# A fused attention block with its block products cut into four column tiles

## The chip, the cores and the metric

The kernel runs on one core of a Trainium2 chip. The metric is the device time of one execution in microseconds (us). Before the change three runs gave 721.99, 722.10 and 722.43 us; their median is 722.1 us. A difference of 0.2% (1.4 us) is about what a measurement of this kernel can tell from no change.

## The reference

The input `x` has 8 batches of 512 positions by 512 channels; `tokens` is one conditioning row for each batch. There are 16 heads of 32 channels.

```python
Q = split_heads(x @ Wq.T + bq);  tQ = split_heads(tokens @ Wq.T + bq)
K = split_heads(x @ Wk.T + bk);  tK = split_heads(tokens @ Wk.T + bk)
V = split_heads(x @ Wv.T + bv)
scores = einsum('bhqd,bhkd->bhqk', Q + tQ, K + tK) / sqrt(32)
out = einsum('bhqk,bhkd->bhqd', softmax(scores, axis=-1), V)
return x + merge_heads(out)
```

Everything is float32.

## The kernel before

**Work units.** A unit `t` is one batch and one group of four heads, 32 units in all (`T`), four to a batch. The four heads of a group lie on the 128 partitions, 32 channels each. A unit needs its q and k turned so that channels lie on partitions (`qkT`, 128 x 512), v with positions on partitions (`vs`), and the row maxima of its scores.

**Four steps for a unit.** The main loop (line 806) runs over the units and does four steps for each, one per chunk `kc` of 128 keys. The instructions of TensorE (PE), VectorE (DVE), ScalarE (ACT) and GpSimd (POOL) run in the order in which they are written; only the order of SyncE's DMA queue (SP) is left to the framework. Each step holds, on PE in this order:

1. `exponentials(t, kc)`: four bf16 matmuls (line 570) that put the negated row maxima into four PSUM banks, and on top of them four float32 matmuls k times q, one for each head (line 573). Each uses 32 rows of the array, so the four heads' row tiles (32\*128) run side by side. ACT turns the banks into `e` (line 584).
2. `row_max(t+1, qc)`: four float32 matmuls q times k of the next unit, again 32\*128 row tiles, into four other banks (line 499). DVE takes the negated maxima of heads 0 and 1 one by one (line 490, 128x512 each) and those of heads 2 and 3 in one instruction over two banks (line 508, 128x1024). ACT then sums the exponentials of these banks for the softmax denominators (`denominators`, line 518), one instruction for each head, which waits for that head's maximum.
3. In steps 0, 2 and 3: half of a projection of the next batch (q in step 0, k in step 2, v in step 3). In step 1: `weighted`, the product of `e` and v for the unit before (line 589, column tiles 128\*32: 128 rows, 32 columns, the four heads side by side), a small product with 16 columns (line 620) and the output.

**A projection in seven products.** A 256-wide half of a projection is a 2 x 2 block product. It is done with seven block products instead of eight, from sums and differences of blocks of x and of W (`xc`, `wc`), listed in `MADE_OF`. `first_products` (odd units) does products 1, 6, half of 2, and 7; `other_products` (even units) does 4, 5, the other half of 2, and 3. Either is seven float32 matmuls of 128 x 128 weights by 256 columns, written at lines 403 (v) and 406 (q, k). The trace lists each float32 matmul as two passes, each with its own weight load: 14 passes for a half. There are 92 such halves in the kernel: 30 for q, 30 for k, 32 for v.

**The small work on a projection.** In `first_products` ACT copies product 1 from PSUM to its place in SBUF (`m1`, line 438), ahead of the denominators. Later DVE adds it to products 6 and 2 (lines 444, 445) and adds product 7 (line 426 for v, 429 for q and k). The last of these releases the bank of product 1. After step 2's maxima, POOL splits them into three bf16 parts (`split_max`, lines 532 to 535) and SP turns them by a DMA transpose (`turn_max`, line 544) for the `exponentials` of the next unit.

**PSUM.** Eight banks are handed out by a table, `TURNS`, one row for a step; `banks(i)` is the i-th bank of the row, `advance()` goes to the next row. A matmul into a bank waits until its last reader is done; the wait sits on its weight load.

Of the kernel before, what the change touches and what calls it, by code (L numbers as in the profile page):

```python
# [12 lines left out]
ALU = mybir.AluOpType  # L13
AX = mybir.AxisListType
# [3 lines left out]
def kernel(  # L18
# [49 lines left out]
    T = B * G  # L68
    HS = S // 2
# [175 lines left out]
    for i in range(NS):  # L245
        r = slice(i * BL, (i + 1) * BL)
# [142 lines left out]

    def block_of_x(b, i, kc, at):  # L390
        f = MADE_OF[i - 1][1]
        if isinstance(f, int):
            return xc[:, f, kc, at]
        off = HS * (f == "22")
        return xT[b][:, kc + 2 * (f != "11"), at.start + off : at.stop + off]

    def product(n, b, u, i, pt, kcs=(0, 1)):

        for kc in kcs:
            w = block_of_w(n, i, u, kc)  # L400
            if n == "v":
                xb = block_of_x(b, i, kc, slice(u * P, (u + 1) * P))
                nc.tensor.matmul(pt, xb, w, start=(kc == kcs[0]), stop=(kc == kcs[-1]))  # L403
            else:
                xb = block_of_x(b, i, kc, slice(0, HS))
                nc.tensor.matmul(pt, w, xb, start=(kc == kcs[0]), stop=(kc == kcs[-1]))  # L406

    def twice(a):
        return a.unsqueeze(1).broadcast_to([P, 2, HS])

    def halves(a):
        return a.rearrange("p (h s) -> p h s", h=2)


    def parts_of(n, b, u):

        if n == "v":
            v = vs[b % 2]
            return v[:, u::2, :HS], v[:, u + 2, :HS], v[:, u::2, HS:], v[:, u + 2, HS:]
        o = pair_of(b * G + u * 2, n)  # L420
        return halves(o[:, 0, :]), o[:, 0, HS:], halves(o[:, 1, :]), o[:, 1, HS:]

    def plus(n, b, u, g, o, pt, rest):

        if n == "v":
            nc.vector.tensor_tensor(o, pt, rest, ALU.add)
        else:
            add = tok[:, "qk".index(n), u * 2 + g, b : b + 1]
            nc.vector.scalar_tensor_tensor(o, pt, add, rest, ALU.add, ALU.add)

    def first_products(n, b, u, dens, small, at, first=0):


        one_, two_ = banks(first), banks(at)
        c1, c12, c2, c22 = parts_of(n, b, u)
        m1 = c2[:, 0, :]
        product(n, b, u, 1, one_[:, :HS])
        nc.scalar.copy(m1, one_[:, :HS])
        dens()
        product(n, b, u, 6, two_[:, :HS])  # L440
        small()
        product(n, b, u, 2, two_[:, HS:], (0,))
        product(n, b, u, 7, one_[:, HS:])
        nc.vector.tensor_tensor(c12, two_[:, :HS], m1, ALU.add)
        nc.vector.tensor_tensor(c1[:, 0, :], two_[:, HS:], m1, ALU.add)
        plus(n, b, u, 1, c22, one_[:, HS:], c12)

    def other_products(n, b, u, dens, small, at):

        dens()  # L450
        one_, two_ = banks(at[0]), banks(at[1])
        product(n, b, u, 4, one_[:, :HS])
        product(n, b, u, 5, one_[:, HS:])
        small()
        product(n, b, u, 2, two_[:, :HS], (1,))
        product(n, b, u, 3, two_[:, HS:])
        c1, c12, c2, c22 = parts_of(n, b, u)
        nc.vector.tensor_tensor(c12, one_[:, HS:], c12, ALU.add)
        nc.vector.tensor_tensor(c2, halves(one_), twice(c22), ALU.add)
        plus(n, b, u, 0, c1, halves(two_), c1)  # L460
        if n != "v":
            for g in range(2):
                qkT[n, b * G + u * 2 + g] = pair_of(b * G + u * 2, n)[:, g, :]

    def project_pair(n, b, r, dens, small, at):

        if b >= B:
            dens()
            small()
        else:  # L470
            (first_products, other_products)[r % 2](n, b, r // 2, dens, small, at)


    nmax = {}
# [4 lines left out]
            nmax[t] = op.tile([P, NS, HG, 1], F32, tag="nmax", name=f"nmax_{t}", bufs=3)  # L479
            sums[t] = op.tile([P, NS, HG, 1], F32, tag="sums", name=f"sums_{t}", bufs=3)  # L480

    def row_max(t, qc):
        if t >= T:
            return
        open_max(t)
        for j in range(HG):
            row_scores(t, qc, j, banks(HG + j))
        if t < T - 2 or t * NS + qc == T * NS - 1:
            for j in range(2):
                nc.vector.tensor_reduce(  # L490
                    nmax[t][:, qc, j : j + 1, 0], banks(HG + j), AX.X, ALU.max, negate=True
                )
        else:
            row_max_of(t, qc, 0, banks(HG, 2))
        row_max_of(t, qc, 1, banks(HG + 2, 2))

    def row_scores(t, qc, j, pt):
        r = slice(j * HD, (j + 1) * HD)
# [8 lines left out]
    def row_max_of(t, qc, pr, pt):  # L507
        nc.vector.tensor_reduce(  # L508
            nmax[t][:, qc, pr * 2 : pr * 2 + 2, 0], pt, AX.X, ALU.max, negate=True
        )  # L510
# [15 lines left out]
    def split_max(t, on=nc.gpsimd):  # L526

        if t >= T:
            return
        m, sp = nmax[t], split[t % 2]  # L530
        rest = op.tile([P, NS, HG, 1], F32, tag="rest", name=f"rest_{t}")
        on.tensor_copy(sp[:, :, :, 0:1], m)
        on.tensor_tensor(rest, m, sp[:, :, :, 0:1], ALU.subtract)
        on.tensor_copy(sp[:, :, :, 1:2], rest)
        on.tensor_tensor(sp[:, :, :, 2:3], rest, sp[:, :, :, 1:2], ALU.subtract)
# [3 lines left out]
    def turn_max(t):  # L539

        if t >= T:
            return
        maxT[t] = op.tile([P, S], BF16, tag="maxT", name=f"maxT_{t}")
        nc.sync.dma_start_transpose(
            maxT[t].rearrange("p (c q) -> p c q", c=NS),
            split[t % 2].rearrange("p c h e -> p (c h e)"),
        )
# [202 lines left out]

    turn[0] = 13
    row_max(0, 0)
    turn_w("v", [1, 2, 3])
    combine_w("v")
# [51 lines left out]
    for t in range(T - 3):  # L806
        b, r = divmod(t, G)

        exponentials(t, 0)
        row_max(t + 1, 1)  # L810
        of = ((t - 1) // G + 1, (t - 1) % G)
        dens = lambda: denominators(t + 1, 1)
        if t:
            project_pair("q", *of, dens, nothing, 1 if r % 2 else (0, 3))
        else:
            first_products("v", 0, 0, dens, nothing, 1)
            turn_x(NC + 2)
            load_residual(1)
        turn_x(t + NC + 3)
        advance()  # L820

        exponentials(t, 1)
        row_max(t + 1, 2)
        dens = lambda: denominators(t + 1, 2)
        if t:
            dens()
            weighted(
                t - 1, banks(0), banks(1), lambda: combine_x(b + 1, r) if r < 2 else None
            )
        else:  # L830
            dens()
            other_products("v", 0, 0, nothing, nothing, (0, 2))
        advance()

        exponentials(t, 2)
        row_max(t + 1, 3)
        split_max(t + 1)
        turn_max(t + 1)
        dens = lambda: denominators(t + 1, 3)
        if t:  # L840
            project_pair("k", *of, dens, nothing, 1 if r % 2 else (0, 3))
        else:
            first_products("v", 0, 1, dens, nothing, 1)
            combine_x(1, 0)
        if t:
            load_residual(t + 1)
        advance()

        exponentials(t, 3)
        row_max(t + 2, 0)  # L850
        dens = lambda: denominators(t + 2, 0)

        project_pair("v", *of, dens, nothing, 1 if r % 2 else (0, 2))
        advance()


# [55 lines left out]
    t = T - 3  # L912
# [21 lines left out]
    t = T - 2  # L934
# [15 lines left out]
    pa, rest = banks(2), [1, 2, 3]  # L950
# [8 lines left out]
    t = T - 1  # L959
# [47 lines left out]
    b, g = divmod(t, G)  # L1007
# [55 lines left out]
```

## Time and profile before

| what | value |
|---|---|
| median of three runs | 722.1 us |
| the profiled execution: its time, its span | 722.59 us, 720.8 us |
| PE busy | 714.2 us (99% of the span), 5296 matmul passes |
| PE weight loads busy | 401.3 us (56%) |
| ACT busy | 617.3 us (86%) |
| DVE busy | 528.0 us (73%) |
| POOL busy | 176.3 us (24%) |
| mean granted TensorE clock | 0.999 |

In the views, `32*128` in front of a shape is rows times columns of the array that a matmul uses, then follow the moving operand's shape and the number of instructions. PEld is the weight load. In a timeline the first number is the start in us from the start of the span and the second the length; a group's length includes the last one's pipeline, so that groups seem to overlap: the pace is read from the differences of starts.

### The profile page before, as it was taken

How to read it: one execution, taken by the hardware profiler on the slowest of the kernel's cores; microseconds unless marked ns; L12 is line 12 of the kernel's file. 1: busy time of each engine (PE TensorE's matmuls, PEld its weight loads, DVE VectorE, ACT ScalarE, POOL GpSimd, SP SyncE). 2: the span in 40 equal slices, each digit the busy share in tenths (PEclk: the TensorE clock that was granted, in tenths of full speed). 3: DMA queues.
4: the chain of work that ended last, by engine and by line, in shares of the span. 5: the costliest groups of instructions: out<-in, count | busy, mean ns of one | idle time of the engine just before them, and what ended most of it. 6: DMA issues, size and time to landing. Idle time of an engine off the chain costs nothing.

```text
span 720.8 us, 14892 instructions
## 1 busy us (share of the span) xinstructions
PE 714.2 (99%) x5296; PEld 401.3 (56%) x5296; DVE 528.0 (73%) x834; ACT 617.3 (86%) x1539; POOL 176.3 (24%) x275
## 2 busy tenths in 40 slices
PE   9999999999999999999999999999999999999997
PEld 7566555565555566555565555565555565555532
DVE  4798777777768777677776877777767767767777
ACT  2589989999899998989999889998989989889674
POOL 3712221122221122221122221122221122221351
PEclk9999999999999999999999999999999999999999
DMA  6733321222322222321322321323201222211211
GB/s 177 110 60 62 53 41 30 49 44 46 53 35 36 50 41 49 53 41 28 51 41 49 52 40 27 53 37 52 38 16 23 38 38 38 37 21 19 37 32 29
DMA packets 223358, 32.91 MB, mean 46 GB/s; under 512 B 221610, under 2 KB 222122, under 8 KB 223284
## 3 DMA queue, kind: packets, MB, share of 16 engines
q1 hardware_dynamic: 221524, 30.92, 25.3%
q10 hardware_dynamic: 1760, 1.05, 0.5%
q8 instruction: 41, 0.67, 0.4%
q14 instruction: 33, 0.27, 0.1%
HBM read 19.75 MB, written 8.39 MB: 39 GB/s over the span
## 4 chain that ended last, share of the span: by engine, by line
PE 97%; DVE 2%; issue 1%; DMA 1%; DVEq 0%
PE psum L406 27%; PE psum L499 16%; PE psum L589 15%; PE psum L403 14%; PE psum L573 14%; PE psum L570 5%; PE psum L350 2%; DVE acc L863 1%; PE psum L889 1%; DMA w_q<-in_L_cond_Wq_dram 1%; PE psum L266 0%; DVE acc L861 0%; PE psum L311 0%; PE psum L667 0%; PE psum L599 0%
## 5 line engine op out<-in xcount | busy, mean ns | idle before, releaser
L518 ACT ACTIVATE dead<-psum,nmax 128x512 f32<-128x512 f32 x480 | 327.6, 702 | 5.1 <-DVE nmax L490 3.1
L584 ACT ACTIVATE e<-psum 128x512 f32<-128x512 f32 x488 | 252.0, 602 | 64.2 <-PE psum L573 63.9
L490 DVE TENSOR_REDUCE nmax<-psum 128x1 f32<-128x512 f32 x240 | 154.5, 686 | 143.1 <-PE psum L499 143.1
L508 DVE TENSOR_REDUCE nmax<-psum 128x2 f32<-128x1024 f32 x130 | 157.7, 1214 | 2.8 <-PE psum L499 2.7
L499 PE MATMUL psum<-kT,qT 32*128 32x512 f32 x1024 | 143.9, 605 | 0.0
L646 POOL TENSOR_TENSOR res<-res,recs 128x512 f32<-128x512 f32 x30 | 31.5, 1049 | 432.1 <-DVE res L645 432.1
L573 PE MATMUL psum<-qT,kT 32*128 32x512 f32 x976 | 125.5, 587 | 0.0
L589 PE MATMUL psum<-e,v 128*32 128x512 f32 x1024 | 121.2, 596 | 0.0
L518 ACT ACTIVATION_READ_ACCUMULATOR dead<-psum,nmax 128x1 f32 x480 | 105.2, 219 | 0.0
L499 PEld LDWEIGHTS psum<-kT,qT 32*128 32x128 f32 x1024 | 59.8, 183 | 58.1 <-ACT dead L518 26.4
L589 PEld LDWEIGHTS psum<-e,v 128*32 128x32 f32 x1024 | 26.6, 110 | 65.1 <-issue 37.6
L573 PEld LDWEIGHTS psum<-qT,kT 32*128 32x128 f32 x976 | 48.6, 185 | 2.2
L403 PE MATMUL psum<-wc_v,xc 128*128 128x256 f32 x192 | 49.3, 379 | 0.0
L570 PE MATMUL psum<-maxT,onesb 3*128 3x512 bf16 x488 | 48.1, 384 | 0.0
L406 PE MATMUL psum<-xc,wc_k 128*128 128x256 f32 x180 | 46.2, 379 | 0.0
L406 PE MATMUL psum<-xc,wc_q 128*128 128x256 f32 x180 | 46.2, 379 | 0.0
L570 PEld LDWEIGHTS <-onesb 3*128 3x128 bf16 x488 | 12.3, 90 | 57.2 <-issue 57.2
L173 POOL TENSOR_TENSOR xr<-xr,bvs 128x512 f32<-128x512 f32 x31 | 39.4, 1272 | 18.7 <-DMA x<-in_x_dram 12.0
L403 PEld LDWEIGHTS psum<-wc_v,xc 128*128 128x128 f32 x192 | 36.5, 190 | 5.0
L647 POOL TENSOR_TENSOR res<-res,xr 128x512 f32<-128x512 f32 x30 | 38.2, 1273 | 2.4
L403 PE MATMUL psum<-wT_v,xT 128*128 128x256 f32 x128 | 37.1, 392 | 0.0
L406 PEld LDWEIGHTS psum<-xc,wc_k 128*128 128x128 f32 x180 | 34.2, 190 | 4.7
(165 smaller groups left out, 791.2 us busy)
## 6 DMA issues: line engine op xcount, KB each, us to landing
xr<-in_x_dram SPq DMA_DIRECT2D x124, 64.0 KB, 2.4
out_dram<-res SPq DMA_DIRECT2D x122, 64.0 KB, 1.9
x<-in_x_dram SPq DMA_DIRECT2D x112, 64.0 KB, 2.4
w_q<-in_L_cond_Wq_dram SPq DMA_DIRECT2D x4, 256.0 KB, 4.4
w_v<-in_L_cond_Wv_dram SPq DMA_DIRECT2D x16, 64.0 KB, 2.4
w_k<-in_L_cond_Wk_dram SPq DMA_DIRECT2D x16, 48.0 KB, 2.3
x<-in_x_dram ACTq DMA_DIRECT2D x2, 256.0 KB, 3.9
x<-in_x_dram SPq DMA_DIRECT2D x2, 256.0 KB, 4.2
```

The lines of the kernel that those rows point to most:

```text
L173: nc.gpsimd.tensor_tensor(xr[t], xr[t], bias, ALU.add)
L403: nc.tensor.matmul(pt, xb, w, start=(kc == kcs[0]), stop=(kc == kcs[-1]))
L406: nc.tensor.matmul(pt, w, xb, start=(kc == kcs[0]), stop=(kc == kcs[-1]))
L490: nc.vector.tensor_reduce(nmax[t][:, qc, j : j + 1, 0], banks(HG + j), AX.X, ALU.max, negate=True)
L499: nc.tensor.matmul(pt, qkT["q", t][r, qc * P : (qc + 1) * P], qkT["k", t][r, :], start=True, stop=True,)
L508: nc.vector.tensor_reduce(nmax[t][:, qc, pr * 2 : pr * 2 + 2, 0], pt, AX.X, ALU.max, negate=True)
L518: nc.scalar.activation(dead, banks(HG + j), AF.Exp, bias=nmax[t][:, qc, j, :], accum_out=sums[t][:, qc, j, :],)
L570: nc.tensor.matmul(bank[j], onesb[r, :], maxT[t][r, :], start=True, stop=False)
L573: nc.tensor.matmul(bank[j], qkT["k", t][r, kc * P : (kc + 1) * P], qkT["q", t][r, :], start=False, stop=True,)
L584: nc.scalar.activation(e[:, i, :], bank[pr * 2 + i], AF.Exp)
L589: nc.tensor.matmul(pt[j * HD : (j + 1) * HD, :], vs[b % 2][:, kc, (g * HG + j) * HD : (g * HG + j + 1) * HD], es[t, kc, j // 2][:, j % 2, ...
L647: nc.gpsimd.tensor_tensor(y, y, xr.pop(t), ALU.add)
```

## The change

`product` issues, instead of one matmul of 128 weight columns, four matmuls of 32 weight columns with the same moving operand, each into its 32 partitions of the same bank. `first_products` in the main loop has DVE copy product 1 instead of ACT, and DVE takes the last two maxima of that step only after this copy, one by one; in step 2 the split and the turn of the maxima follow them. The two `first_products` of unit 0 and those ahead of the loop keep ACT's copy. In even units the order stays as it was.

```diff
@@ product
-                xb = block_of_x(b, i, kc, slice(u * P, (u + 1) * P))
-                nc.tensor.matmul(pt, xb, w, start=(kc == kcs[0]), stop=(kc == kcs[-1]))
+                still, moving = block_of_x(b, i, kc, slice(u * P, (u + 1) * P)), w
             else:
-                xb = block_of_x(b, i, kc, slice(0, HS))
-                nc.tensor.matmul(pt, w, xb, start=(kc == kcs[0]), stop=(kc == kcs[-1]))
+                still, moving = w, block_of_x(b, i, kc, slice(0, HS))
+            for j in range(HG):
+                r = slice(j * HD, (j + 1) * HD)
+                nc.tensor.matmul(
+                    pt[r], still[:, r], moving, start=(kc == kcs[0]), stop=(kc == kcs[-1])
+                )
@@ first_products
-    def first_products(n, b, u, dens, small, at, first=0):
+    def first_products(n, b, u, dens, small, at, first=0, held=None):
...
         product(n, b, u, 1, one_[:, :HS])
-        nc.scalar.copy(m1, one_[:, :HS])
+        if held:
+            nc.vector.tensor_copy(m1, one_[:, :HS])
+            held()
+        else:
+            nc.scalar.copy(m1, one_[:, :HS])
         dens()
@@ project_pair
-    def project_pair(n, b, r, dens, small, at):
+    def project_pair(n, b, r, dens, small, at, held):
+        if r % 2:
+            held()
         if b >= B:
             dens()
             small()
-        else:
-            (first_products, other_products)[r % 2](n, b, r // 2, dens, small, at)
+        elif r % 2:
+            other_products(n, b, r // 2, dens, small, at)
+        else:
+            first_products(n, b, r // 2, dens, small, at, 0, held)
@@ row_max
+    def one_max(t, qc, j, pt):
+        nc.vector.tensor_reduce(
+            nmax[t][:, qc, j : j + 1, 0], pt, AX.X, ALU.max, negate=True
+        )
+
-    def row_max(t, qc):
+    def row_max(t, qc, hold=False):
...
-        row_max_of(t, qc, 1, banks(HG + 2, 2))
+        last, both = [banks(HG + 2), banks(HG + 3)], banks(HG + 2, 2)
+
+        def held():
+            if hold and t < T - 2:
+                for j in range(2):
+                    one_max(t, qc, 2 + j, last[j])
+            else:
+                row_max_of(t, qc, 1, both)
+
+        if hold:
+            return held
+        held()
+        return nothing
@@ the main loop, step 0 (step 3 likewise)
-        row_max(t + 1, 1)
+        held = row_max(t + 1, 1, r % 2)
...
-            project_pair("q", *of, dens, nothing, 1 if r % 2 else (0, 3))
+            project_pair("q", *of, dens, nothing, 1 if r % 2 else (0, 3), held)
@@ the main loop, step 2
-        row_max(t + 1, 3)
-        split_max(t + 1)
-        turn_max(t + 1)
+        rest = row_max(t + 1, 3, r % 2)
+
+        def held():
+            rest()
+            split_max(t + 1)
+            turn_max(t + 1)
+
...
-            project_pair("k", *of, dens, nothing, 1 if r % 2 else (0, 3))
+            project_pair("k", *of, dens, nothing, 1 if r % 2 else (0, 3), held)
```

The product matmuls grow from 644 to 2576, in 14 x 4 passes instead of 14 for a half. 42 copies of product 1 move from ACT to DVE, and 42 maxima over two banks become 84 over one bank. On SP the framework puts two DMAs of `xr` instead of one ahead of the DMA transpose of the maxima in odd units.

More of the change, by code (lines that the diff above doesn't have):

```diff
@@ L489, in row_max @@
             for j in range(2):
-                nc.vector.tensor_reduce(
-                    nmax[t][:, qc, j : j + 1, 0], banks(HG + j), AX.X, ALU.max, negate=True
-                )
+                one_max(t, qc, j, banks(HG + j))
         else:
             row_max_of(t, qc, 0, banks(HG, 2))
-        row_max_of(t, qc, 1, banks(HG + 2, 2))
+        last, both = [banks(HG + 2), banks(HG + 3)], banks(HG + 2, 2)
[9 more added lines that the diff above has]
+        return nothing
     def row_scores(t, qc, j, pt):
@@ L835 @@
         exponentials(t, 2)
-        row_max(t + 1, 3)
-        split_max(t + 1)
-        turn_max(t + 1)
+        rest = row_max(t + 1, 3, r % 2)
[3 more added lines that the diff above has]
+            turn_max(t + 1)
         dens = lambda: denominators(t + 1, 3)
         if t:
-            project_pair("k", *of, dens, nothing, 1 if r % 2 else (0, 3))
+            project_pair("k", *of, dens, nothing, 1 if r % 2 else (0, 3), held)
         else:
+            held()
             first_products("v", 0, 1, dens, nothing, 1)
@@ L849 @@
         exponentials(t, 3)
-        row_max(t + 2, 0)
+        held = row_max(t + 2, 0, r % 2)
         dens = lambda: denominators(t + 2, 0)
-        project_pair("v", *of, dens, nothing, 1 if r % 2 else (0, 2))
+        project_pair("v", *of, dens, nothing, 1 if r % 2 else (0, 2), held)
         advance()
```

## The prediction

> **What bounds the kernel.** I read the page first: busy shares, then the chain that ended last.
>
> ```profile
> PE 714.2 (99%) x5296; PEld 401.3 (56%) x5296; DVE 528.0 (73%) x834; ACT 617.3 (86%) x1539; POOL 176.3 (24%) x275
> ...
> PE 97%; DVE 2%; issue 1%; DMA 1%; DVEq 0%
> PE psum L406 27%; PE psum L499 16%; PE psum L589 15%; PE psum L403 14%; PE psum L573 14%; PE psum L570 5%; PE psum L350 2%; DVE acc L863 1%; PE psum L889 1%; DMA w_q<-in_L_cond_Wq_dram 1%; PE psum L266 0%; DVE acc L861 0%; PE psum L311 0%; PE psum L667 0%; PE psum L599 0%
> ```
>
> PE is the bound nearly everywhere, and 41% of the chain (L406 and L403) are the products that the change cuts. What a pass costs, and what lies between passes, is seen in the timeline of PE from 300 to 318 us:
>
> ```profile
> 301.05 1.12 PE L499 MATMUL psum<-kT,qT 32*128 32x512 f32 x8
> 302.10 1.13 PE L403 MATMUL psum<-wT_v,xT 128*128 128x256 f32 x4
> 303.07 1.03 PE L403 MATMUL psum<-wc_v,xc 128*128 128x256 f32 x4
> 303.93 0.59 PE L403 MATMUL psum<-wT_v,xT 128*128 128x256 f32 x2
> 304.36 1.03 PE L403 MATMUL psum<-wc_v,xc 128*128 128x256 f32 x4
> 305.32 0.40 PE L570 MATMUL psum<-maxT,onesb 3*128 3x512 bf16 x4
> ...
> 306.41 1.11 PE L499 MATMUL psum<-kT,qT 32*128 32x512 f32 x8
> ...
> 311.75 1.03 PE L499 MATMUL psum<-kT,qT 32*128 32x512 f32 x8
> 312.71 1.07 PE L589 MATMUL psum<-e,v 128*32 128x512 f32 x8
> 313.59 0.23 PE L620 MATMUL psum<-apart,modulo 128*32 128x16 f32 x8
> 313.65 2.76 PE L589 MATMUL psum<-e,v 128*32 128x512 f32 x24
> 316.35 0.40 PE L570 MATMUL psum<-maxT,onesb 3*128 3x512 bf16 x4
> ```
>
> From the differences of starts: four passes of 256 columns take 0.97 us when they are the first after L499 (302.10 to 303.07) and 0.863 later (303.07 to 303.93; 216 ns a pass). The column tiles of L589 are the model for the changed products. Their four heads run side by side: 24 passes, six rounds of four, in 2.69 us; 430 ns a round of 512 columns, so 215 for 256. **The cut therefore saves nothing on a pass**, a pass in four column tiles being one round.
>
> The grouped lines, shapes kept apart, say the same of the entry: a group that holds first passes has a longer mean (25 ns over four passes, 12.5 over eight: about 104 ns for each first one).
>
> ```profile
> L403 PE MATMUL psum<-wc_v,xc 128*128 128x256 f32 x192 | 49.3, 379 | 0.0
> L403 PE MATMUL psum<-wT_v,xT 128*128 128x256 f32 x128 | 37.1, 392 | 0.0
> L403 PE MATMUL psum<-wT_v,xc 128*128 128x256 f32 x64 | 18.1, 405 | 0.0
> ```
>
> Last the timeline of all engines around 306.4, for what PE waits for:
>
> ```profile
> 306.11 0.22 ACT L518 ACTIVATION_READ_ACCUMULATOR dead<-psum,nmax 128x1 f32 x1
> 306.38 0.21 PEld L499 LDWEIGHTS psum<-kT,qT 32*128 32x128 f32 x4 [0.22 <-ACT dead L518]
> 306.41 0.68 PE L499 MATMUL psum<-kT,qT 32*128 32x512 f32 x4
> ```
>
> ACT ends its last denominator at 306.33; PE's weight load for that bank goes 0.05 later, too late to hide under the pass before, and L499 takes 1.04 us (306.41 to 307.44) instead of 0.956 (311.75 to 312.71).
>
> **Part 1, the column tiles.** *Entry:* 104 ns of a 128-column weight load are exposed at the first pass (0.967 - 0.863). For L589 eight passes from 312.710 to 313.593 are two rounds in 0.883, against 0.859: 24 ns, a 32-column load. Saved: 80 ns. *Exit:* from the last four product passes to L570 0.96 us (304.36 to 305.32) less 0.863, 0.096; from the last six rounds of L589 to L570 2.694 less 6 x 0.4295, 0.117. The four tiles start some 7 ns apart, and the last one ends 20 ns later. Lost: 20 ns. *Between passes:* four 32-column loads (110 ns each, side by side) must hide under 213 ns of matmul instead of 427. The 128-column load of 190 ns does so now. I take nothing. Net 60 ns for each of the 92 halves: **5.5 us**.
>
> One kind does not pass it all on. In step 2 of even units DVE's last operation (L429, 751 ns) releases the bank that L499 waits for; it starts 0.09 after the last product pass, and DVE's own queue would let it start only 0.04 earlier. Off: 15 x 0.02, **0.3 us**.
>
> **Part 2, ACT loses its copy, DVE gets it.** Starts of L499 to the next group, over the main loop: 0.955 where nothing is late; 1.057 after a q `first_products` (14 times), 1.051 after k (14), 1.037 after v (16, 14 of them changed), and 1.040 after k `other_products` (15, DVE's case above, which stays). The first three end in ACT, as in the last fence. In place of a copy and four denominators ACT has only the denominators. The copy takes 0.27 us of ACT's time from start to next start (330.19 to 330.46); in a v step ACT also waits 0.1 for product 1. ACT ends 0.27 (q, k) to 0.37 us (v) earlier. The wait costs 0.08 to 0.10, and the faster products take 0.06 more, so about 0.1 us is left over and the wait is gone: 14 x 0.102 + 14 x 0.096 + 14 x 0.082 = **3.9 us**.
>
> *What is late next: DVE.* In the v step at 301 it now starts maxima at 302.17 and 302.78, the double one at 303.37, then L444 at 304.63, L445 at 304.97 and L426 at 305.43, where it waits for product 7. After: copy at 303.37 (product 1 ends near 303.2), two maxima at 303.71 and 304.31 (a copy is taken as L444, 0.34 from start to start; a maximum is 0.60), L444 at 304.91, L445 at 305.26, L426 at 305.60, end 306.03. With 0.05 for the semaphore PE's load may go at 306.08. It must go by 306.41 - 0.14 (what parts 1 and 2 save in the step) - 0.107 (the load) = 306.16. 0.08 us to spare; by the same sum 0.08 in k (the bank is the first that L499 needs) and 0.06 in q. Behind the copy on DVE the third and fourth maximum are late for ACT's third and fourth denominator: ready at 304.5 and 305.1, wanted at 304.5 and 305.2. Product 7 writes the bank that the copy reads and now waits for DVE (303.8 with the semaphore; its load is due at 303.95). So this edit costs nothing as long as DVE's copy is no more than 0.06 us longer than I take it; from there each 0.1 us costs at most 42 x 0.1 = 4.2 us. The other end is DVE's 128x512 copy (L314, 692 ns against 424 for L444; 0.27 longer): about 8 us back. I take the nearer row, of equal size and source.
>
> *Step 2 of odd units:* the maxima end about 0.4 us later, and POOL's four splits (0.25 us each) and the turn follow; on SP one more `xr` DMA (0.53) stands ahead of the turn. Turns are issued near +5.0 us after the step's L499 and land 2.4 later; L570 wants them at +9.5. Two microseconds of cover shrink to one. One turn was issued at +6.2 (302.0): it would be late by about 0.1. I take 0. Nothing else that PE waits for in this step stands behind them on POOL or SP.
>
> **Sum.** 5.5 - 0.3 + 3.9 = 9.1 us. The profiled execution took 722.59 us (span 720.8, 1.8 around it), 0.5 above the median of 722.1. Against its own time 713.5; against the median **713.0 us**, 1.3% less.
>
> **A rule that speaks against it.** In L589 and L620 the loads of the next round, 110 ns long, lie under the running passes: rounds keep to 430 ns. The Trainium skill ("TensorE: Matmul & The Clock Gate", Part 3, "The mechanism") says a weight load overlaps running matmuls only when its row group differs; column tiles share all rows. By that, each of 92 x 14 rounds would show 24 ns of load: 31 us more, some 744 us. The rows disagree, and I go by them.
>
> **Rivals.** *A, slower: PE can't issue the tiles fast enough.* A pass now is four loads and four matmuls in 216 ns, 54 ns a pair. No long stretch of this trace is as dense: the weighted step has 60 pairs in 5.7 us, 95 ns each. For it: when matmuls are tiny (L707, ten columns at 7.4 us) pairs come 62 ns apart. At 62 ns a round takes 248 ns: 92 x 14 x 32 ns = 41 us, less the 9 gained: 754 us. Against it: eight pairs of L620 start in 0.06 us, and the loads of L707 have 128 columns, which explains their pace. It decides from 223 ns a round on (9.1 us / 1288 rounds = 7 ns). The same threshold holds if four streams reading one moving operand at the same place hinder each other; L589's four streams read four places, and the trace has no row for one.
> The same page (Part 1, "Wait — 56ns, not 53.3ns?") gives 62 ns per matmul as the issue cost when hardware decode is off; that would be rival A's price.
> *B, DVE takes ACT's place.* If the copy or the waits on DVE are 0.15 us longer, the 3.9 us stay as a wait on DVE: 717 us.
> *C, nothing gained:* the entry is set by the switch of tile shape and not by the load's width; then 5.5 us fall away, 718 us; with B too, 722 us. L589's entry speaks against it.
>
> **Chances.** The forecast's case 0.65 (its own range 710.5 to 715.5: the exit free, +1.8 us; the copy longer, or some turns late, -2); B or C 0.12 (716 to 719); within 0.2% of 722.1, 0.05; A or hindered streams 0.18 (724 to 755). The range from 709.5 to 724 leaves out most of A. Faster 0.77, same 0.05, slower 0.18.
>
> **What would show it.** Right: product passes keep a pace of 215 ns a round; the first round after L499 is 24 ns longer, not 104; L499 lasts 0.955 after odd units' steps; ACT's busy time falls by 42 copies, some 16 us; DVE's rises by some 24 us (42 x 0.42 and 42 x 0.16). Wrong: rounds above 220 ns (A); L499's loads released by DVE L429 or L426 (B); a first round still 100 ns longer (C).

## The result

The changed kernel takes 716.83 us (median of 4 runs, 716.06 to 718.08) against 722.05 us before (4 runs, 721.89 to 722.43): ratio 0.9929, 95% interval 0.9915 to 0.9942. It is 5.2 us faster; the forecast was 9.1 us faster (713.0). The time lies in the stated range of 709.5 to 724, but 3.8 us of the expected gain did not come. The profiled execution took 717.11 us, with a span of 715.0. TensorE had its full clock in both traces (0.998 in the changed kernel, 0.999 before).

The page of the changed kernel, busy shares and the chain that ended last:

```profile
PE 705.7 (99%) x9160; PEld 321.1 (45%) x9160; DVE 535.3 (75%) x918; ACT 604.7 (85%) x1497; POOL 176.5 (25%) x275
...
PE 93%; DVE 2%; DMA 2%; issue 1%; ACT 1%; POOL 0%; SPq 0%; DVEq 0%; POOLq 0%
PE psum L407 39%; PE psum L526 16%; PE psum L616 15%; PE psum L600 14%; PE psum L597 5%; PE psum L350 2%; DMA maxT<-split 1%; DVE acc L894 1%; PE psum L920 1%; DMA w_q<-in_L_cond_Wq_dram 1%; PE psum L266 0%; DVE nmax L535 0%; DVE acc L892 0%; PE psum L694 0%; PE psum L311 0%
```

PE is the bound as before, but its share of the chain has fallen from 97% to 93%, and a transfer that was not in the chain of before stands in it now: `maxT<-split`, the turn of the maxima (L571), with about 1%. That is the first hint of where the missing part went.

The products themselves look as forecast. The timeline of PE in the changed kernel, a first half of q (start, length, engine, line, operation, how many):

```profile
303.54 1.02 PE L526 MATMUL psum<-kT,qT 32*128 32x512 f32 x8
304.50 1.07 PE L407 MATMUL psum<-xc,wT_q 128*32 128x256 f32 x16
305.38 1.05 PE L407 MATMUL psum<-xc,wc_q 128*32 128x256 f32 x16
306.25 0.61 PE L407 MATMUL psum<-xT,wT_q 128*32 128x256 f32 x8
306.68 1.05 PE L407 MATMUL psum<-xT,wc_q 128*32 128x256 f32 x16
307.66 0.39 PE L597 MATMUL psum<-maxT,onesb 3*128 3x512 bf16 x4
```

Sixteen tile passes are four rounds: 0.863 us where they are not the first (305.38 to 306.25), so 216 ns a round, as one wide pass took. Behind the scores (L526) they take 0.89 (304.496 to 305.384): 24 ns of entry where there were 104. The half takes 3.162 us from its first pass to L597; before it was 3.222. The scores that start it take 0.955 us (303.541 to 304.496); in this kind of step they took 1.04 to 1.06.

The waits of TensorE's weight loads in the changed kernel (engine, line waited at, releaser; us in all, times, longest):

```profile
PEld psum L526 <- ACT dead L545: 16.9, 45, 0.8
...
PEld psum L526 <- DVE qT L432: 8.0, 14, 0.6
PEld psum L526 <- DVE kT L432: 6.5, 15, 0.7
PEld L597 <- DMA maxT<-split: 5.6, 10, 1.2
```

and of the kernel before:

```profile
PEld psum L499 <- ACT dead L518: 26.4, 89, 0.8
```

The scores' loads wait for ACT 45 times where they waited 89 times: ACT has let go of the 42 steps that the change touches. In the last line for the changed kernel loads wait for the turn, ten times and up to 1.2 us; no load waited for it before. One of them, in the timeline of the changed kernel:

```profile
340.96 0.51 SPq L165 DMA_DIRECT2D xr<-in_x_dram  x1
341.57 1.19 SPq L571 DMA_TRANSPOSE maxT<-split  x1
...
344.21 1.05 PE L407 MATMUL psum<-wc_v,xc 128*32 128x256 f32 x16
...
345.94 0.10 PEld L597 LDWEIGHTS <-onesb 3*128 3x128 bf16 x4 [1.16 <-DMA maxT<-split]
```

The turn leaves SP at 341.57, lands 4.32 us later instead of the usual 2.5, and L597 starts 0.75 us late: this half takes 3.908 us and not 3.162. The half at 84.77 is late in the same way (3.694; its turn lands after 4.26 us). A third one, at 128.03 (3.323), is late for another reason:

```profile
124.22 3.29 SPq L677 DMA_DIRECT2D out_dram<-res  x4
126.77 0.27 POOL L562 TENSOR_TENSOR split<-rest,split 128x16 bf16<-128x16 f32 x1
127.55 1.04 SPq L165 DMA_DIRECT2D xr<-in_x_dram  x2
128.70 1.19 SPq L571 DMA_TRANSPOSE maxT<-split  x1
131.35 0.10 PEld L597 LDWEIGHTS <-onesb 3*128 3x128 bf16 x4 [0.57 <-DMA maxT<-split]
```

This turn lands 2.61 us after its issue, near the usual, but it is issued 1.67 us after the split: the four stores of a result ahead of it on SP took 3.29 us to issue where one usually takes 0.5. The three halves together cost 1.44 us.

To compare kernels I add up two things over each trace, from the starts of PE's groups: the 89 product halves that end in the product over the sums (L407 to L597; the other three halves of the 92 end elsewhere), and the 146 groups of scores (L526 to the next group). A turn counts as late when its last part lands over 3.2 us after its issue. Each trace is one execution, and how many turns are late, and which, can differ in another.

| | packets of PE's instructions | late turns of 29 | products, us | scores, us | last matmul at | median, us | less than before in the same batch |
|---|---|---|---|---|---|---|---|
| before | 41 | 2 | 286.67 | 124.57 | 716.30 | 722.05 | |
| changed | 72 | 8 | 282.83 | 121.71 | 709.38 | 716.83 | 5.2 |
| tiles alone | 72 | 7 | 281.40 | 127.47 | 713.30 | 720.28 | 2.0 |
| copy and maxima alone | 41 | 2 | 287.14 | 120.72 | 712.68 | 719.35 | 2.9 |
| changed, 64 columns | 51 | 2 | 284.37 | 121.28 | 710.33 | 716.66 | 5.6 |
| changed, tiles at the entry only | 46 | 5 | 299.90 | 120.62 | 725.68 | 732.11 | -9.8 |
| changed, maxima as a pair | 71 | 8 | 282.24 | 133.57 | 722.33 | 727.96 | -5.6 |
| changed, k step as before | 71 | 6 | 281.58 | 123.63 | 710.30 | 716.61 | 5.8 |
| changed, no turn | 71 | none | 281.39 | 121.42 | 707.33 | 714.31 | 8.1 |
| before, no turn | 41 | none | 286.68 | 124.90 | 716.28 | 723.09 | -0.7 |

### The profile page after: what moved, and what is told of

Same layout as the page of the kernel before. It is cut to its first block, busy times and chain, and to the rows that moved or that the text cites. A ratio compares the mean times of both kernels' runs of the same rounds, so it can differ in the third digit from the quotient of the medians.

```text
span 715.0 us, 22748 instructions
## 1 busy us (share of the span) xinstructions
PE 705.7 (99%) x9160; PEld 321.1 (45%) x9160; DVE 535.3 (75%) x918; ACT 604.7 (85%) x1497; POOL 176.5 (25%) x275
## 4 chain that ended last, share of the span: by engine, by line
PE 93%; DVE 2%; DMA 2%; issue 1%; ACT 1%; POOL 0%; SPq 0%; DVEq 0%; POOLq 0%
PE psum L407 39%; PE psum L526 16%; PE psum L616 15%; PE psum L600 14%; PE psum L597 5%; PE psum L350 2%; DMA maxT<-split 1%; DVE acc L894 1%; PE psum L920 1%; DMA w_q<-in_L_cond_Wq_dram 1%; PE psum L266 0%; DVE nmax L535 0%; DVE acc L892 0%; PE psum L694 0%; PE psum L311 0%
## 5 line engine op out<-in xcount | busy, mean ns | idle before, releaser
L494 DVE TENSOR_REDUCE nmax<-psum 128x1 f32<-128x512 f32 x324 | 208.3, 685 | 133.4 <-PE psum L526 133.4
L526 PE MATMUL psum<-kT,qT 32*128 32x512 f32 x1024 | 141.1, 598 | 0.0
L535 DVE TENSOR_REDUCE nmax<-psum 128x2 f32<-128x1024 f32 x88 | 106.8, 1215 | 2.7 <-PE psum L526 2.7
L545 ACT ACTIVATION_READ_ACCUMULATOR dead<-psum,nmax 128x1 f32 x480 | 107.8, 225 | 0.0
L526 PEld LDWEIGHTS psum<-kT,qT 32*128 32x128 f32 x1024 | 59.5, 182 | 55.9 <-ACT dead L545 16.9
L407 PE MATMUL psum<-wc_v,xc 128*32 128x256 f32 x768 | 50.2, 379 | 0.0
L597 PE MATMUL psum<-maxT,onesb 3*128 3x512 bf16 x488 | 48.1, 385 | 1.2 <-DMA maxT<-split 1.1
L407 PE MATMUL psum<-xc,wc_k 128*32 128x256 f32 x720 | 47.1, 379 | 0.0
L407 PE MATMUL psum<-xc,wc_q 128*32 128x256 f32 x720 | 47.1, 379 | 0.0
L597 PEld LDWEIGHTS <-onesb 3*128 3x128 bf16 x488 | 12.3, 91 | 65.7 <-issue 60.2
L407 PE MATMUL psum<-wT_v,xT 128*32 128x256 f32 x512 | 36.8, 382 | 0.0
L407 PE MATMUL psum<-xT,wT_k 128*32 128x256 f32 x480 | 34.5, 382 | 0.0
L407 PE MATMUL psum<-xT,wT_q 128*32 128x256 f32 x480 | 34.5, 382 | 0.0
```

Source lines behind the costliest of these rows:

```text
L407: nc.tensor.matmul(pt[r], still[:, r], moving, start=(kc == kcs[0]), stop=(kc == kcs[-1]))
L494: nc.vector.tensor_reduce(nmax[t][:, qc, j : j + 1, 0], pt, AX.X, ALU.max, negate=True)
L526: nc.tensor.matmul(pt, qkT["q", t][r, qc * P : (qc + 1) * P], qkT["k", t][r, :], start=True, stop=True,)
L535: nc.vector.tensor_reduce(nmax[t][:, qc, pr * 2 : pr * 2 + 2, 0], pt, AX.X, ALU.max, negate=True)
L545: nc.scalar.activation(dead, banks(HG + j), AF.Exp, bias=nmax[t][:, qc, j, :], accum_out=sums[t][:, qc, j, :],)
L597: nc.tensor.matmul(bank[j], onesb[r, :], maxT[t][r, :], start=True, stop=False)
```

## The experiments

The theory after the result: both terms of the sum are right, and the missing part is the turn, which the forecast costed at nothing. Its new place took its cover, and the many more instructions of PE make it land late more often. The rivals: the parts lean on each other and do not add up; the entry does not go with the width of the load, or its price is wrong; VectorE is the new bound.

### The parts alone

The tiles alone (the kernel before, with the loop over column tiles):

```diff
-                nc.tensor.matmul(pt, w, xb, start=..., stop=...)
+            for j in range(HG):
+                r = slice(j * HD, (j + 1) * HD)
+                nc.tensor.matmul(pt[r], still[:, r], moving, start=..., stop=...)
```

> The kernel before with the 32-column tiles alone; the copy stays on ScalarE and the maxima stay where they were. If the two parts lean on each other: the tiles save 0.06 us at each of 92 entries, but in the 42 steps whose next scores wait for ScalarE the shorter stream only waits longer, so 50 x 0.06 = 3.0 less 0.3 for VectorE, 719.4 us; the group of score products after a first half has its 1.04 to 1.06 us and grows by up to 0.06. If the parts simply add: 5.2 less, 716.9. If the tiles are worth nothing alone: 722.1. The turn of the maxima is issued at its old place, so although some 70 packets of instructions are fetched, as in the changed kernel, its late landings (about 4.2 us for 2.4) are covered by the old slack of about 2.1 us and stop nothing.

Measured: 720.28 us, ratio 0.9975 (0.9966 to 0.9984); 719.4 was expected if the parts lean on each other. The products give 5.27 us back in full, and the scores take 2.90 of it away. Where the group behind a first half of k took 1.051 us it takes 1.111: the 60 ns by which the stream is shorter are waited away. The waits of this kernel:

```profile
PEld psum L502 <- ACT dead L521: 23.6, 73, 0.8
...
PEld L573 <- DMA maxT<-split: 2.1, 5, 0.4
```

ACT still holds the scores 73 times. Seven turns land late here too, but the longest half is 3.171 us: they fall into the old cover and cost 0.01 us together. So in this trace 72 packets of instructions cost nothing while the turn keeps its old place. The trace is of the fastest of ten runs, which spread over 2.1 us (719.61 to 721.75); what the slower ones lost is not shown.

The copy on VectorE with the held maxima alone (the changed kernel with wide products):

```diff
-            for j in range(HG):
-                r = slice(j * HD, (j + 1) * HD)
-                nc.tensor.matmul(pt[r], still[:, r], moving, start=..., stop=...)
+                nc.tensor.matmul(pt, w, xb, start=..., stop=...)
```

> The changed kernel with products 128 columns wide again: only VectorE's copy between the held maxima is left. By the steps on record: 42 x about 0.09 = 3.9 less, 718.2 us; the scores after a first half at 0.955 us; first product passes to the sums' product 3.22 us as before. About 41 packets of instructions as before. If late turns come from the fetches, only two or three of the 29 turns land later than 3 us, and the turn's shrunken cover costs at most 0.3. If they come from the new place of the turn, some nine land late, as in the changed kernel, and the gain falls to about 2.5 (719.6). If VectorE takes ScalarE's place: 722.

Measured: 719.35 us, ratio 0.9958 (0.9944 to 0.9971), 1.2 us above the 718.2 expected. The scores fall by 3.85 us (forecast 3.9), and the groups behind a first half stand at 0.955 in the median. Two turns land late, as before; one of them costs 0.46 us (a half of 3.682). The last matmul is 3.6 us earlier, the median 2.9 lower.

The two gains of the parts alone (2.0 and 2.9) come to 4.9, close to the 5.2 of both together, but that is chance: in the traces the parts are not independent. The 2.90 us that ACT takes from the tiles come back once the copy is gone, and what the two together should give is lost elsewhere.

### The width of the tiles

```diff
-            for j in range(HG):
-                r = slice(j * HD, (j + 1) * HD)
+            for j in range(2):
+                r = slice(j * 2 * HD, (j + 1) * 2 * HD)
```

> The changed kernel with two tiles of 64 columns in place of four of 32. If the width of the first load sets the entry: about 53 ns exposed where it was 24, some 10 ns lost at the exit where it was 20, so about 0.02 us more at each of 92 entries, 1.8 in all, less half of the 1.4 us that late turns cost (some 50 to 55 packets of instructions in place of 72, about five late turns): 717.9 us, where the changed kernel has 716.9. If the switch to another stream sets the entry and not the width: the same entry of 24 ns, 716.2. A round takes 0.216 us in any case.

Measured: 716.66 us, ratio 0.9920 (0.9908 to 0.9933). A half takes 3.175 us. The first round behind the scores takes 0.266 us (305.061 to 305.327), so 50 ns of entry, between 24 and 104. The second tile starts 7 ns behind the first, the fourth of four 20 ns. Entry and stagger make 104, 57 and 44 ns for 128, 64 and 32 columns, and the halves differ by just that: 3.222, 3.175, 3.162. So the entry goes with the width of the first load (the number of tiles changes with it, and no run moves the one without the other). The time is not the 717.9 of this theory but that of the changed kernel: the halves are 1.2 us longer in all, but only two turns are late (they still cost 1.8 us, the longer half 4.233), and VectorE's waits (below) are 0.4 smaller.

### Tiles at the entry only

If only the first load is exposed, four narrow tiles at the start of a half should do:

```diff
+            tiles = HG if entry and kc == kcs[0] else 1
-            for j in range(HG):
-                r = slice(j * HD, (j + 1) * HD)
+            for j in range(tiles):
+                r = slice(j * P // tiles, (j + 1) * P // tiles)
```

> The changed kernel with column tiles at the first block of the first product of each half alone (products 1 and 4, their first block); all other products are 128 columns wide. If only the first load of a half is exposed, and a wide load still hides beneath the four narrow tiles before it: the entry saves the same 80 ns, the 20 ns of the exit are lost once behind the narrow tiles instead, and the passes to the sums' product take 3.16 us as in the changed kernel; about 45 packets of instructions in place of 72, two or three late turns in place of nine: 716.9 less 1.2, 715.7 us. If the wide load cannot hide there, about 0.08 us comes back at each of 92 entries: 723. If late turns do not follow the number of fetches: 716.9 as the changed kernel.

Measured: 732.11 us, ratio 1.0134 (1.0120 to 1.0148). The rival is right, and more: a half takes 3.359 us, 0.197 more than with tiles throughout. The weight loads of this kernel at a half's start:

```profile
306.46 0.16 PEld L408 LDWEIGHTS psum<-wT_v,xT 128*32 128x32 f32 x8 [0.76 <-ACT e L612]
307.03 0.30 PEld L408 LDWEIGHTS psum<-wT_v,xT 128*128 128x128 f32 x2 [0.41 <-issue]
307.35 0.62 PEld L408 LDWEIGHTS psum<-wc_v,xc 128*128 128x128 f32 x3
```

The wide load follows only at 307.03, 0.309 us behind the last narrow tile (306.722) where a pass takes 0.216: the narrow tiles run out first, 93 ns. The next wide pass follows 0.320 us later and not 0.216 (307.031 to 307.351): 104 ns, the entry of a wide load again. So the price belongs to the switch from one tile shape to another, twice: about 0.09 us to run out and a load whose width counts. Each half pays one switch more than with tiles throughout, 92 x 0.197 = 18.1 us, less what the longer halves spare in late turns and in the scores (120.62 us for 121.71). Five turns land late with 46 packets, where two or three were expected.

### The maxima one by one

```diff
-            if hold and t < T - 2:
+            if False:
```

> The changed kernel with its held maxima taken as a pair by one instruction, as before, after VectorE's copy. If it is the maxima one by one that let ScalarE go on: the third denominator starts when the pair ends, about 0.42 us later than now (339.33 in the profile of after, against about 339.75), and the next scores' banks come free later by as much; what ScalarE has in hand there is 0.1 to 0.3 us, so the scores after a first half stand at 1.05 to 1.25 us in place of 0.955 in 42 steps: 721 to 728 us, I take 723. If the copy's move alone took ScalarE off the path: 717, the same as the changed kernel.

Measured: 727.96 us, ratio 1.0079 (1.0066 to 1.0092), beyond the 723 I took and at the end of the range. The scores behind a first half of k stand at 1.272 us, behind v at 1.192. The timeline of this kernel shows why:

```profile
301.23 1.22 DVE L535 TENSOR_REDUCE nmax<-psum 128x2 f32<-128x1024 f32 x1
...
302.56 0.69 ACT L545 ACTIVATE dead<-psum,nmax 128x512 f32<-128x512 f32 x1 [0.33 <-DVE nmax L535]
...
303.24 0.68 ACT L545 ACTIVATE dead<-psum,nmax 128x512 f32<-128x512 f32 x1
...
303.55 0.81 PEld L526 LDWEIGHTS psum<-kT,qT 32*128 32x128 f32 x8 [0.37 <-DVE kT L432]
```

ACT idles 0.33 us for the pair and the last denominator ends at 303.81 + 0.20, past the start of the scores that need its bank. The copy's move without the split of the pair would be a loss of 5.6 us: the two belong together.

### The turn's place

The k step back as it was (the pair, the split and the turn first; ACT copies), the rest changed:

```diff
-        rest = row_max(t + 1, 3, r % 2)
-        def held(): ...
+        row_max(t + 1, 3)
+        split_max(t + 1)
+        turn_max(t + 1)
...
-            project_pair("k", ..., held)
+            project_pair("k", ..., None if r % 2 else nothing)
```

> The changed kernel with the k step of a first half put back as it was (the pair of maxima, the split and the turn first, ScalarE copies); the q and v steps stay changed. If late turns cost what the trace says because the new place took a microsecond of their cover: late landings of about 4 us stay as frequent (72 packets of instructions), but no product half is longer than 3.2 us, 1.4 us less; ScalarE's wait comes back in 14 steps, where the tiles alone had 1.111 us for 0.955, 2.2 us more: 717.6 us. If the place of the turn has nothing to do with it: the long halves of 3.3 to 3.9 us stay, 719.1.

Measured: 716.61 us, ratio 0.9921 (0.9908 to 0.9934). Six turns land late, but the products need 281.58 us, 1.25 less than in the changed kernel; the longest half has 3.343 us, above the 3.2 expected. In exchange the scores behind a first half of k are at 1.111, as forecast, and the scores take 1.9 us more. The place of the turn is thus what makes late landings cost. The trace of the changed kernel says the same: of its eight late turns six stand in even units, where the turn kept its place, and cost nothing (0.15 to 0.70 us to spare); the two in odd units cost 0.53 and 0.75 us. In the k step the change wins from ACT about what it loses to the turn.

Then the residual loads were taken out of the turn's way on SP:

```diff
-                nc.sync.dma_start(
+                nc.gpsimd.dma_start(
                     xr[t][h * BL : (h + 1) * BL], spread(x[b], g * P + h * BL)
```

> The changed kernel with the four residual loads of a unit issued by GpSimd, behind the split of the maxima, so that they no longer stand ahead of the turn on SP. If SP's row of transfers in odd units makes up part of the lost cover: the turn leaves SP at most 0.1 us after the split (0.3 to 1.7 now), the slack of odd units goes from 1.33 to about 1.8 us, a landing of 4.2 us costs at most 0.1, and 1.0 to 1.4 us is won: 715.7 us. If the loads on GpSimd hold up what stands behind them there (the bias, the rows of the sums, the next result), a new wait on GpSimd shows in the chain, and the time is 717 to 722.

> Two tiles of 64 columns and the residual loads on GpSimd together. By sums over the traces: a product half of 3.175 us for 3.162, 1.2 us more over 92, VectorE's two stalls 0.4 less, 51 packets of instructions in place of 72 and the turn covered, 1.4 less: 716.3 us, and a narrower spread of runs than the 2.0 us of the changed kernel. If the loads on GpSimd hold up the work there: 717 to 722, as for the kernel with 32 columns.

Measured: 728.42 us, ratio 1.0086 (1.0073 to 1.0099), with four tiles; 720.81, ratio 0.9981 (0.9972 to 0.9990), with two. Both expectations fell, and not for the reason that the rival gave. Three groups of the page with four tiles (busy time, mean ns | idle time before, what ended most of it) and a line of its transfers (KB each, median us to landing):

```profile
L165 POOL DMA_DIRECT2D xr<-in_x_dram x124 | 80.7, 658 | 0.0
L173 POOL TENSOR_TENSOR xr<-xr,bvs 128x512 f32<-128x512 f32 x31 | 39.4, 1271 | 84.8 <-DMA xr<-in_x_dram 81.6
L597 PE MATMUL psum<-maxT,onesb 3*128 3x512 bf16 x488 | 48.1, 385 | 14.4 <-DMA maxT<-split 14.3
...
xr<-in_x_dram POOLq DMA_DIRECT2D x124, 64.0 KB, 3.1
```

GpSimd waits for its loads, but PE, DVE and ACT wait no longer for GpSimd than in the changed kernel (2.3 us in all, and 2.2). It is the turn that is late: over all 29 turns its median landing goes from 2.5 to 4.3 us (3.9 with two tiles); the list of transfers, which dates 17 of the 29, has 5.0 and 3.8. The four loads now start behind the split in the same moment as the turn (from 0.1 us before it to 1.8 us after it, most of them). PE waits 14.3 us for it. The Trainium skill ("DMA: Bandwidth & Descriptors", "Issuing engines are not separate DMA queues") says that transfers started by different engines run on the same 16 DMA engines and interleave; these runs agree, with 2.5 us against 4.3. Why two tiles suffer less than four I did not find out. A version that keeps the loads on SP, but all of them behind the turn, was not run.

### Without the turn

The cost of the turn by itself: the products over the sums read a tile of zeros.

```diff
-        maxT[t] = op.tile([P, S], BF16, tag="maxT", name=f"maxT_{t}")
-        nc.sync.dma_start_transpose(maxT[t]..., split[t % 2]...)
+        maxT[t] = flat
```

> The changed kernel without the turn of the maxima: the products over the sums read a tile of zeros set once, so the maxima that are split are turned by nobody and the weights are not shifted by them. Everything else is issued as before. If late turns cost what the trace of after says: no product half above 3.17 us, 1.4 us less than the changed kernel, 715.4, and a spread of runs of about 0.6 us in place of 2.0. If the long halves have another cause that lies beside the turn: 716.8, and halves of 3.3 to 3.9 us stay. VectorE's waits behind a second half (1.071 and 0.981) stay in both.

> The kernel before without the turn, in the same way. Its turns stop nothing in its trace, except 0.1 us in all, so 722.2 us, as with the turn. If a transfer of that kind costs something by itself, beside its lateness (its place in SP's row, its traffic): less than 721.5.

Measured: the changed kernel 714.31 us (714.22 to 715.03), ratio 0.9889 (0.9875 to 0.9902) to the kernel before; the kernel before 723.09 us, ratio 1.0007 (0.9998 to 1.0016), that is, no faster. Without the turn the changed kernel is 2.5 us faster than with it, the kernel before is not; the changed kernel's runs spread over 0.8 us where they spread over 2.0; and no half of it exceeds 3.162 us. From the kernel before without the turn to the changed kernel without it are 8.8 us in the medians and 8.95 in the last matmul (716.28 to 707.33), against the 9.1 of the forecast.

### VectorE behind a second half

```diff
-        one_, two_ = banks(at[0]), banks(at[1])
-        product(4); product(5); small(); product(2, (1,)); product(3)
-        c12 += ...; c2 = ...; c1 = ...
+        two_, one_ = banks(at[0]), banks(at[1])
+        product(2, (1,)); product(3); small(); product(4); product(5)
+        c1 = ...; c12 += ...; c2 = ...
```

> The changed kernel without the turn, and with the second half of a projection in another order: products 2 and 3 and the block that they complete first, products 4 and 5 and theirs last; the same products and sums. If the scores behind a second half wait because VectorE's last sum there makes the block that they read: the scores at 1.071 us (behind k's second half, 15 times) go to about 0.96, those at 0.981 (behind q's) to 0.955, 1.7 + 0.4 = 2.1 us less than the changed kernel without the turn, 713.3. If VectorE is late there as a whole, so that whatever it does last is waited for: 715.4, no change.

Measured: 727.16 us, ratio 1.0063 (1.0049 to 1.0077), 12.9 us more than without the new order. The gain did not come, but the run does not decide between the two theories, as its waits show. The timeline of this kernel behind a second half of q:

```profile
354.99 0.74 DVE L434 SCALAR_TENSOR_TENSOR qT<-psum,tok,qT 128x512 f32<-128x512 f32 x1
...
355.97 0.42 DVE L468 TENSOR_TENSOR qT<-psum,qT 128x256 f32<-128x256 f32 x1 [0.24 <-ACT dead L547]
...
356.31 0.68 DVE L469 TENSOR_TENSOR qT<-psum,qT 128x512 f32<-128x512 f32 x1
...
357.05 0.31 PEld L528 LDWEIGHTS psum<-kT,qT 32*128 32x128 f32 x8 [0.84 <-DVE qT L469]
```

The scores' load goes at 357.05, right behind L469 (356.31 + 0.68). These scores read no block of the pair that is being made here; they are those of the next unit, whose q and k were made earlier. What ties them to L469 is the bank: the edit swaps the banks of the two blocks too, so the sum that now comes last again reads the bank that the first head's scores write, and two sums stand behind the last product where it was one. Behind a second half of v it is the bank as well: 15 times the load of the fourth head waits for the sum L469 of v, which the scores do not read at all, and these scores go from 0.955 to 1.232 us. Behind a second half of k:

```profile
105.78 0.42 DVE L468 TENSOR_TENSOR kT<-psum,kT 128x256 f32<-128x256 f32 x1 [0.24 <-ACT dead L547]
106.12 0.68 DVE L469 TENSOR_TENSOR kT<-psum,kT 128x512 f32<-128x512 f32 x1
106.31 0.83 PEld L528 LDWEIGHTS psum<-kT,qT 32*128 32x128 f32 x8 [0.31 <-issue]
```

Here the scores do read the k just made. Their first load goes at 106.31, after L468 (its end at 106.20) and while L469 still runs; the third head's load waits for L469, which reads that head's bank. L468 adds product 5 to `c12`, the second half of the block `c1`, so the new order does not complete this block early: it needs L468, behind product 5, as before. The edit therefore left both the block and the bank to the last products, and whether scores whose block and bank are free early would gain the 2.1 us stays open.

## Why the prediction was right, and where it was not

*A pass gains nothing, the entry 80 ns, the exit loses 20: right.* 216 ns a round, 24 ns of entry, 3.222 to 3.162 us a half. Without the turn's disturbance the 89 halves give 5.28 us and the three others 0.18, together 5.46 against 5.5.

*The loads hide under the passes: right.* Four loads of 110 ns go under each running round, and the rounds keep to 216 ns. The rule of the Trainium skill that was weighed against it ("TensorE: Matmul & The Clock Gate", Part 3, "The mechanism"), that a load overlaps only matmuls of another row group, does not describe these column tiles; the measurement decides. By the same rows rival A is out: eight instructions in 216 ns over whole halves.

*ACT lets go of 42 steps, 3.9 us: right.* The copy alone takes 3.85 us off the scores, and the wait did not move to DVE in these steps (rival B): they stand at 0.955. The chain of slacks of 0.06 to 0.08 us held, though just: with the maxima as a pair it breaks.

*"Off: 15 x 0.02, 0.3 us": too small.* The step named only the scores behind k's second half (1.041 to 1.071 us; the 15 together 15.53 to 15.96, so 0.4 lost). Those behind q's second half wait for the same line of DVE and went from 0.956 to 0.982, 14 times, 0.4 us more. Both follow the length of the half: medians of 1.041, 1.058, 1.071 and 0.956, 0.968, 0.982 for 3.222, 3.175, 3.162 us. The term is 0.8 and not 0.3, with the turn and without it.

*"One turn was issued at +6.2 (302.0): it would be late by about 0.1. I take 0.": this is the step that failed.* The loss of cover was seen, and put at one of two microseconds. In five of the 14 odd units that is right: 1.33 to 1.43 us are left. In seven the turn leaves SP more than 0.8 us after the split (0.84 to 1.68), which two of the 29 did before the change. Each of the seven stands behind a store whose issue took 1.0 to 1.84 us instead of 0.5, with a packet of instructions under way. One of them is 0.16 us late (128.03), near the 0.1 that the step names; the other six have 0.09 to 0.90 to spare. In the last two odd units the landing itself is late, 4.26 and 4.32 us after the issue, and that is most of the cost. So what the step missed is that landings far above 2.4 us exist, two in the trace of before (3.47 and 4.14), and that the change itself makes them, and slow issues ahead of the turn, more frequent. It cost 1.4 us in the trace and about 2.5 us in the medians.

*The starting point.* 1.1 us of the profiled execution's time lie behind its last matmul (5.6 us to the end of the span, 4.5 in the trace of before); the other traces of the table have 4.5 to 4.9, so I count it as that execution's own. The sum also carried over 1.8 us of time outside the span, which all 46 runs of before in the experiments have. In the changed kernel it is 2.1 to 2.8 in the four runs, and 2.1 to 2.4 without the turn: 0.3 us or more of the missing time lies outside the span, for a cause that was not looked for.

*The signs.* Rounds, first round and scores came as written. ACT's busy time fell by 12.6 us and not 16, DVE's rose by 7.3 and not 24: I had added mean durations, but records of neighbours overlap. With overlaps counted once the 42 copies are 13.9 us, the maxima 2.8, and the records of the sums behind them shrink by about 9.

So the likeliest case was the right one in mechanism, though 716.83 lies outside the 710.5 to 715.5 that the prediction gave to it and inside the 716 to 719 of rivals B and C: the time alone would have pointed to them. Rival C fell with the widths (104, 57, 44 ns). Of the 3.8 us that are missing some 2.5 are the turn and 0.5 DVE behind second halves; of the remaining 0.8 some 0.3 to 0.5 lie outside the span, and the rest is within the spread of the runs. No version tried beats the changed kernel by more than its measurement can tell: 64 columns (716.66) and the k step as before (716.61) equal it.

## What to carry to other kernels

When a change multiplies an engine's instructions, look at the packets of instructions in the list of DMA queues, and then at every short transfer whose cover the change shortens: what landed in time in the profile before may land 2 us late in one turn out of four, or be issued late behind a slow neighbour in its queue. A load is dear where the tile shape changes, by the width of the first load and the running out of what was there, so use one shape for a whole stretch or not at all. And a gain in front of an engine that is 0.1 us late is only paid out when that engine is taken off the path as well: the tiles alone kept 2.4 of their 5.3 us.

## What the runs showed of the hardware

The late turns follow the fetches of PE's own instructions. The list of DMA queues counts them, in the changed kernel (packets, MB, share):

```profile
q8 instruction: 72, 1.18, 0.7%
```

and in the kernel before:

```profile
q8 instruction: 41, 0.67, 0.4%
```

A packet is 16 KB and there is one for some 256 of PE's matmuls and weight loads: 10592 and 41 before, 13168 and 51 with 64 columns, 18320 and 72 in the changed kernel. The Trainium skill ("Runtime: NRT & Kernel Launch", "Instruction fetch mechanics") says the same of the block, 16 KiB for 256 instructions, and that the cost of crossing into the next is mostly hidden. For PE that is so here. For the transfers it is not: a packet takes 0.9 to 1.7 us of a DMA engine. The turn's 16 parts show it. In the turn of 341.57 fifteen land by 2.42 us and the sixteenth at 4.32; a packet runs from 1.93 to 3.22 us after the issue. Where the packet starts 1.2 to 1.8 us after the issue, even the last six parts land together at 3.8 to 4.4 us (191.03, 276.55, 448.35, 619.39). Where it starts 2.26 us after the issue or later, the turn is in time in this kernel (six cases); with 64 columns one such turn, its packet at 2.33, landed after 4.78. In the changed kernel all 8 late turns had a packet under way within 2.45 us of their issue, and of the 21 others 6. Over the eight kernels with turns and loads on SP it is 38 of 40 late turns, and 24 of 192 others. Other transfers show the same: all 19 issues on SP of the changed kernel, after its first 20 us, that took over 0.9 us (the usual is 0.5) overlap a packet, and of the 354 shorter ones 29. No run moved the packets alone, so the cause rests on these coincidences and on the parts that land singly; that the late turns cost the time was shown by taking the turn away.
